# Layer 0's x_proj product ahead of TensorE's other work in slot 6, and three PSUM banks for the first image of the last layer

## The chip, the cores and the metric

The kernel runs on one core of one Trainium2 chip. A core has five engines that each work through their own queue in order: TensorE (PE in the profile, with its weight loads as PEld), VectorE (DVE), ScalarE (ACT), GpSimd (POOL) and SyncE (SP), which here only issues transfers between HBM and the on-chip memory SBUF. TensorE writes its results to PSUM[...]. The metric is the device time of one execution in microseconds; lower is better. Before the change it is 8299.07 us, the median of three runs (8296.89 to 8299.89).

## The reference

The network has four layers on four images of 64 x 64 positions with 128 channels, each of the form `x = x + layer(group_norm(x))`, all in float32. The change touches layer 0, a selective scan over the image in four directions k, and the beginning of layer 3, attention over a 7 x 7 neighbourhood. Layer 0, cut to what matters here:

```python
x_dbl = einsum('bkdl,kcd->bkcl', xs, x_proj_weight)          # x_proj: 256 channels -> 8 + 16 + 16
dts, Bm, Cm = split(x_dbl, [R, R + N], axis=2)               # R = 8, N = 16
delta = softplus(einsum('bkrl,kdr->bkdl', dts, dt_projs_weight) + bias)
A = -exp(A_logs)
def step(h, xs):                                             # 4096 steps, 16 states for each channel
    ut, dt, bt, ct = xs
    h = exp(dt[..., None] * A) * h + (dt * ut)[..., None] * bt[:, :, None, :]
    return h, einsum('bkdn,bkn->bkd', h, ct)
```

Layer 3: `qkv = x @ qkv_w.T + qkv_b` on the normalised image, then for every position the softmax over its 49 neighbours of `q . k * scale + bias`, the weighted sum of their `v`, and a projection.

## The kernel before

Layer 0 walks through 128 units (image b, direction k in the order 1, 3, 0, 2, chunk c of 512 positions), each of 16 slots, one for each state n. In a slot GpSimd makes `dB`, ScalarE makes the two halves of `dA`, VectorE runs the two scans, TensorE transposes a quarter of an older group of `h` into `pt`, ScalarE copies it to `hT`, and TensorE multiplies the `hT` of the slot before into `yT`. Here are the slot's loop, and the generator that prepares the next unit's delta:

```python
def inputs(k, c, u, par):
    xd_ps = spare("xd_ps")[0:48, :]
    for s in range(2):
        nc.tensor.matmul(xd_ps, lhsT=w_x[:, s, k, :], rhs=u[:, s, :], start=(s == 0), stop=(s == 1))
    yield
    xd = xds[c % 2]
    nc.scalar.copy(xd[0:24, :], xd_ps[0:24, :])
    yield
    Ct = tmp.tile([48, 32, 16], F32, name="Ct")[32:48]
    nc.scalar.copy(Ct, xd_ps[32:48, :].rearrange("n (a t) -> n t a", t=32))
    ...                                        # stores of xd and Ct to HBM
    yield bd, Wd
    ...                                        # delta: dp = w_dt . xd, exp, ln, min/max; du
spare = lambda name: psm.tile([P, CH], F32, name=name, tag="m")     # one bank, for all side work
...
for n in range(NS):
    slot = NS * i + n
    ...
    nc.gpsimd.tensor_tensor(dB, du, B_now[...], ALU.mult)
    flush("dve")
    if i + 1 < len(units) and n in (9, 11):
        next(coming)
    for s in range(2):
        dA = psx.tile([P, CH], F32, name="dA", tag="x")             # three banks
        nc.scalar.activation(dA, delta[:, s, :], AF.Exp, scale=A_neg[:, k, s, n : n + 1])
        nc.vector.tensor_tensor_scan(h[:, s, :, q], dA, dB[:, s, :], state[:, s, n : n + 1], ALU.mult, ALU.add)
        if s == 0 and i + 1 < len(units):
            if n in (7, 8, 10):
                next(coming)
        elif n == 7 and i + 1 < len(units):
            bd_next, Wd_next = next(coming)
        flush(f"act{s}")
    copy = transposed() if slot >= LAG else (lambda: None)          # LAG = 7
    copy()
    flush("act2")
    ...
    if i + 1 < len(units):
        if n == 1:
            u_next, v_next = fetch(*units[i + 1])
        if n == 6:
            coming = inputs(*units[i + 1][1:], v_next, (i + 1) % 2)
        if n in (6, 7, 9):
            next(coming)
        if n == 13:
            ready = next(coming)
```

What `transposed` puts into the queues: eight transposes, then the yT products of the slot before; the copy of `pt` comes last. `pt` has a single buffer (two banks).

```python
pt = ps.tile([P, 4, 2, P], F32, name="pt")
for j in range(4):
    for s in range(2):
        nc.tensor.transpose(pt[:, j, s, :], G["h"][...], sh.ident)
if todo is not None:
    products(*todo)                            # four products of hT (slot before) into yT
hT = tmp.tile([P, 4, 2 * P], F32, name="hT")
return lambda: nc.scalar.copy(hT, pt.rearrange("p j s d -> p j (s d)"))
```

Beside this the loop carries side work in small pieces: preparing the next image (norm, the z product, a 3 x 3 convolution as nine products) and finishing the last one. Its TensorE results go through the same spare bank, and its other parts are put off with `later`, to a place in a later slot; `flush` puts them into the queues there. The convolution starts in slot 11 and ends with its ninth product in slot 3 of the next unit. What follows it is `silu`, with `wait = (0, 1, 2)` for a convolution and `(0, 0, 1)` for z:

```python
def silu(v, bias, minus, dst, later, wait):    # v is the spare bank
    e = tmp.tile([P, CH], F32, name="e", tag="t2", bufs=4)
    def product():
        nc.vector.scalar_tensor_tensor(e, v, bias, e, ALU.add, ALU.mult)
        nc.sync.dma_start(dst, e)
    later("act0", nc.scalar.activation, e, v, AF.Exp, scale=-1.0, bias=minus)
    later("act1", nc.scalar.activation, e, e, AF.Ln, bias=1.0, slots=1 + wait[0])
    later("act0" if wait[1] else "act2", nc.scalar.activation, e, e, AF.Exp, scale=-1.0, slots=1 + wait[1])
    later("dve", product, slots=1 + wait[2])
    return e
```

So the `product` of a convolution is put into VectorE's queue at the head of slot 6. Behind it, in slot 7, ScalarE copies `e` by columns (`xw`).

Layer 2 takes its SBUF in pools that are stacked in the order of their creation, and layer 3's pools are stacked on the same addresses once layer 2 is done:

```python
pools = pool("l2big", 1), pool("l2tmp", 1), pool("l2small", 1), ps      # layer 2; big holds x, z, m, sp: 7 x 16 KB
...
wp = pool("l3w", 1)                            # layer 3: weights, two padded images kp, zero
big, tmp, small = pool("l3big", 2), pool("l3tmp", 2), pool("l3small", 4)
psS, psT = pool("l3psS", 2, space=PSUM), pool("l3psT", 2, space=PSUM)
psO, psM = pool("l3psO", 1, space=PSUM), pool("l3psM", 1, space=PSUM)
```

Layer 3 prepares an image in `front(b)`: transpose and statistics (`pg`), normalise, values (`pv`), keys (`pk`). Of the first image all pieces run before anything else; those of the others are spread over the attention steps of the image before. `queries` takes `pq` from the same bank.

```python
def front(b):
    x = big.tile([P, NJ, DM], F32, name="x3")
    load_image(nc, x, x_in(b))
    ...
    for c in range(NCH):
        pg = psM.tile([P, CH], F32, name="pg3", tag="m")
        for q in range(4):
            nc.tensor.transpose(pg[:, q * P : (q + 1) * P], x[:, 4 * c + q, :], sh.ident)
        nc.vector.bn_stats(st[:, c, :], pg)
        nc.scalar.copy(xn[:, c * CH : (c + 1) * CH], pg)
        yield
    s_, o_ = sh.group_scale(st, psM, small, "m")
    ...                                        # xn = xn * s_ + o_ in two halves on VectorE
    for c in range(NCH):
        pv = psM.tile([P, 4, P], F32, name="pv3", tag="m")
        ...                                    # four products xn . w_v
        vt = tmp.tile([P, 4, P], F32, name="vt")
        tt(vt, pv, w["v_b"].unsqueeze(1).to_broadcast([P, 4, P]), ALU.add)
        ...                                    # two stores of vt into the padded v in HBM
        yield
    for c in range(NCH):
        pk = psM.tile([P, CH], F32, name="pk3", tag="m")
        nc.tensor.matmul(pk, lhsT=w["qkv"][:, P : 2 * P], rhs=xn[:, c * CH : (c + 1) * CH], start=True, stop=True)
        nc.scalar.activation(kps[b % 2][...], pk.rearrange("p (h w) -> p h w", w=64), AF.Identity, bias=...)
        yield
...
for _ in front(0):
    pass
rows = {0: queries(0, 0)}
for s in range(NU + 6):                        # attention steps; ps = psS.tile([P, 2, CH]) from step 0 on
    ...
```

Of the kernel before, what the change touches and what calls it, by code (L numbers as in the profile page):

```python
# [2 lines left out]

# [7 lines left out]
F32 = mybir.dt.float32  # L11
# [5 lines left out]
P = 128  # L17
# [5 lines left out]
CH = 512  # L23
# [59 lines left out]
def layer0(sh, A, x_in, x_out, scr):  # L83
# [7 lines left out]
    with ExitStack() as ctx:  # L91
        pool = lambda name, bufs, **kw: ctx.enter_context(tc.tile_pool(name=name, bufs=bufs, **kw))
        wp = pool("l0w", 1)
        tmp = pool("l0tmp", 2)
        small = pool("l0small", 2)
# [361 lines left out]
        with tc.manual_schedule(engines=order):  # L457
            for i, (b, k, c) in enumerate(units):
                if i % per == 0:
                    ln_st = small.tile([P, NJ, 1, 6], F32, name="ln_st")  # L460
                    if b + 1 < NB:
                        sides.insert(0, Side(before(b + 1, spare, later), 17 + 8 * 23, NS * i, 28 * NS))
                rev = k >= 2
                pc = NCH - 1 - c if rev else c
                dst = lambda n, pc=pc, b=b: tiles(scr(f"y2{b % 2}" if n == 2 else f"y{n}")[pc * CH : (pc + 1) * CH, :])
                delta, du = ready
                if c == 0:
                    state = small.tile([P, 2, NS], F32, name="state")
                    nc.gpsimd.memset(state, 0.0)
                unit = dict(k=k, rev=rev, pc=pc, u=u, yT=[None, None], started=set(), st=ln_st, dst=dst)  # L470
                Ws = unit["Ws"] = {}
                coming = None
                for n in range(NS):
                    slot = NS * i + n
                    g, q = divmod(n, 4)
                    if q == 0:
                        B_now = Bb
                        if g < 3:
                            Bb = broadcast(bd, g + 1)
                        elif i + 1 < len(units):  # L480
                            Bb = broadcast(bd_next, 0)
                        h = tmp.tile([P, 2, CH, 4], F32, name="h", bufs=3)
                        G = dict(unit=unit, g=g, h=h, q=0)
                    dB = tmp.tile([P, 2, CH], F32, name="dB", bufs=3)
                    nc.gpsimd.tensor_tensor(dB, du, B_now[:, q : q + 1, :].to_broadcast([P, 2, CH]), ALU.mult)  # L485
# [4 lines that stand above are left out]
                        dA = psx.tile([P, CH], F32, name="dA", tag="x")  # L490
                        nc.scalar.activation(dA, delta[:, s, :], AF.Exp, scale=A_neg[:, k, s, n : n + 1])  # L491
                        nc.vector.tensor_tensor_scan(  # L492
                            h[:, s, :, q], dA, dB[:, s, :], state[:, s, n : n + 1], ALU.mult, ALU.add
# [4 lines that stand above are left out]
                        elif n == 7 and i + 1 < len(units):  # L498
                            bd_next, Wd_next = next(coming)
                        flush(f"act{s}")  # L500
                    copy = transposed() if slot >= LAG else (lambda: None)
                    copy()
                    flush("act2")
                    if q == 2:
                        W = Ws[g] = tmp.tile([P, 32, 16], F32, name="W", bufs=4)
                        nc.sync.dma_start(W, Wd[g, 0 : P * CH].rearrange("(p t a) -> p t a", p=P, a=16))
                    if q == 3:
                        queue.append(G)
                        if c < NCH - 1:
                            later("act1", nc.scalar.copy, state[:, :, 4 * g : 4 * g + 4], h[:, :, CH - 1, :], slots=5)  # L510

                    if i + 1 < len(units):
                        if n == 1:
                            u_next, v_next = fetch(*units[i + 1])
                        if n == 6:
                            coming = inputs(*units[i + 1][1:], v_next, (i + 1) % 2)
                        if n in (6, 7, 9):
                            next(coming)
                        if n == 13:
                            ready = next(coming)  # L520

                    if n == 10:
                        y = unit["y"] = tmp.tile([P, 4, 2 * P], F32, name="y", tag="t4", bufs=4)
                        if k == 0:
                            src = scr("y3").rearrange("(w q r) d -> r w q d", w=64, r=2)
                            for r in range(2):
                                nc.sync.dma_start(y[64 * r : 64 * r + 64], src[r, :, 4 * c : 4 * c + 4, :])
                        elif k != 1:
                            nc.sync.dma_start(y, dst(1 if k == 3 else 0))

                    inside = [d for d in sides if d.inside]
                    free = n not in BUSY and not inside and slot >= taken
                    able = dict(f=False, l=False, m=free, n=free and n != 5, z=free and n != 5, c=free and n == 11)
                    for d in inside or [d for d in sides if able[d.need] and d.due(slot)][:1]:
                        taken = slot + dict(m=1, n=2, z=2, c=3)[d.need]
                        d.free_at = slot + 1
                        d.step()
                    for d in sides:
                        if d.need in ("f", "l") and d.due(slot):
                            if d.need == "l":  # L540
                                d.free_at = slot + 3
                            d.step()
                    sides = [d for d in sides if d.need]
                if i + 1 < len(units):
                    u, bd, Wd = u_next, bd_next, Wd_next
                if i % per == per - 1:
                    slot += 1
                    if b + 1 < NB:
                        for d in sides:
                            d.finish(flush_all)  # L550
                    if b + 1 < NB:
                        sides = [Side(after(b, ln_st, later, range(NCH)), 8 * 6, NS * (i + 1) + 8, (28 if b + 2 < NB else 22) * NS)]
                elif b == NB - 1 and i % per == 3 * per // 4:

                    done = [NS * (i + 1 + n) + 8 for n in range(NCH)]
                    sides.append(Side(after(b, ln_st, later, range(NCH - 1, -1, -1)), 8 * 6, done[0], 1, done))
            while queue or copied:
                transposed()()
            for d in sides:
                d.finish(flush_all)  # L560
# [816 lines left out]
def layer2(sh, w, wp, x_in, x_out, scr, wt):  # L1377
    tc, nc = sh.tc, sh.nc
    with ExitStack() as ctx:
# [5 lines left out]
                nc.vector.memset(t, 0.0)  # L1385
        for t in w["XG"]:
            nc.vector.memset(t[:, 4, 64:65], 1.0)
        pools = pool("l2big", 1), pool("l2tmp", 1), pool("l2small", 1), ps
        paced = copy(sh)
        paced.nc = Pace(nc)  # L1390
        engines = {mybir.EngineType.PE, mybir.EngineType.Activation, mybir.EngineType.DVE, mybir.EngineType.Pool}
# [12 lines left out]
def layer3(sh, A, x_in, out, v_pads):  # L1404
# [5 lines left out]
    with ExitStack() as ctx:  # L1410
# [31 lines left out]

        def front(b):

            x = big.tile([P, NJ, DM], F32, name="x3")
            load_image(nc, x, x_in(b))
            xn = big.tile([P, NT], F32, name="xn3")
# [1 line left out]
            yield  # L1449
            st = small.tile([P, NCH, 6], F32, name="gn_st", bufs=2)  # L1450
            for c in range(NCH):
                pg = psM.tile([P, CH], F32, name="pg3", tag="m")
                for q in range(4):
                    nc.tensor.transpose(pg[:, q * P : (q + 1) * P], x[:, 4 * c + q, :], sh.ident)
                nc.vector.bn_stats(st[:, c, :], pg)
                nc.scalar.copy(xn[:, c * CH : (c + 1) * CH], pg)
                yield
# [4 lines left out]
                nc.vector.tensor_scalar(xc, xc, s_, o_, ALU.mult, ALU.add)  # L1462
            yield
            for c in range(NCH):
                pv = psM.tile([P, 4, P], F32, name="pv3", tag="m")
                for q in range(4):
                    nc.tensor.matmul(
                        pv[:, q, :],
# [9 lines left out]
                    nc.sync.dma_start(rows[r], vt[64 * r : 64 * r + 64])  # L1478
                yield
            for c in range(NCH):  # L1480
                pk = psM.tile([P, CH], F32, name="pk3", tag="m")
                nc.tensor.matmul(
                    pk, lhsT=w["qkv"][:, P : 2 * P], rhs=xn[:, c * CH : (c + 1) * CH], start=True, stop=True
                )
                nc.scalar.activation(
                    kps[b % 2][:, 3 + 8 * c : 11 + 8 * c, 3:67],
                    pk.rearrange("p (h w) -> p h w", w=64),
                    AF.Identity,
                    bias=w["qkv_b"][:, 1:2],
                )  # L1490
                yield
# [343 lines left out]
```

## Time and profile before

| stage | from, us | to, us | PE busy, us | DVE busy, us | ACT busy, us | POOL busy, us | granted PE clock |
|---|---|---|---|---|---|---|---|
| layer 0 | 0 | 5938 | 4719 | 5382 | 5287 | 5127 | 0.98 |
| end of layer 0 | 5938 | 6046 | 67 | 74 | 66 | 61 | 0.88 |
| layer 1 | 6046 | 6640 | 515 | 302 | 151 | 0 | 0.91 |
| layer 2 | 6640 | 7692 | 764 | 565 | 340 | 101 | 0.82 |
| entry of layer 3 | 7692 | 7777 | 45 | 15 | 11 | 2 | 0.50 |
| layer 3 | 7777 | 8299 | 462 | 415 | 374 | 191 | 0.97 |

The table is the profile's busy time by window, with the windows set at the first and last instructions of the layers. In every profile line below, `L379` is a line of the kernel, `pt<-ident,h` says what is written and what is read, `x8` is how many instructions the line sums up, and what stands in brackets or behind the bar is how long the engine sat idle just before it and who ended that. The idle time of an engine that isn't the bound costs nothing. So the reading goes from the engine that is busiest in a stage to what it waits for, and from there to the order of the queues.

### The profile page before, as it was taken

What the parts mean: (1) busy time and instruction counts of PE and PEld (TensorE: products, weight loads), DVE (VectorE), ACT (ScalarE), POOL (GpSimd) and SP (SyncE); (2) the same over time, 40 slices, a digit from 0 to 9 for tenths busy, and PEclk for the clock granted to TensorE, in tenths of its full rate; (3) what the DMA queues carried; (4) which work ended last, traced back from release to release, by engine and by line L of the source; (5) the groups of instructions that cost most, each with busy time, mean ns of one, the idle gap of its engine ahead of it and who ended that gap; (6) DMA issues with size and microseconds to landing.
All of it is one profiled execution on the core that took longest, in us unless ns stands there. A gap on an engine that the chain in (4) does not pass through costs nothing.

```text
span 8299.4 us, 140501 instructions
## 1 busy us (share of the span) xinstructions
PE 6571.5 (79%) x52976; PEld 4171.0 (50%) x52976; DVE 6753.8 (81%) x7948; ACT 6229.0 (75%) x10246; POOL 5482.7 (66%) x2502
## 2 busy tenths in 40 slices
PE   7788888778788877888877777787779878686689
PEld 3444454444445444444544444454467766464456
DVE  2889999998999999889999999999944545645578
ACT  3899999989899898989988999999822213315467
POOL 0889889988888898888889999999800011020233
PEclk9899999999999999999999999999989988788799
DMA  6445555445555544455555445455442041331332
GB/s 127 153 143 188 162 164 176 158 156 166 176 168 172 173 165 161 157 169 168 176 179 170 157 156 185 174 174 181 148 103 43 23 118 35 87 101 31 96 94 79
DMA packets 1281977, 1163.78 MB, mean 140 GB/s; under 512 B 637973, under 2 KB 1075825, under 8 KB 1214354
## 3 DMA queue, kind: packets, MB, share of 16 engines
q1 hardware_dynamic: 1279618, 1153.06, 44.0%
q8 instruction: 417, 6.83, 0.3%
q14 instruction: 262, 2.15, 0.1%
q10 hardware_dynamic: 1680, 1.74, 0.1%
HBM read 962.66 MB, written 189.74 MB: 139 GB/s over the span
## 4 chain that ended last, share of the span: by engine, by line
PE 21%; ACT 11%; DVE 11%; issue 3%; DMA 2%; POOL 2%; SPq 1%; DVEq 0%; ACTq 0%; POOLq 0%
DVE h L492 4%; ACT hT L389 4%; ACT dA L491 4%; PE pt L379 2%; PE po L695 1%; PE pf L690 1%; POOL dB L485 1%; PE pz L883 1%; PE pu L883 1%; PE pt L1518 1%; DVE in_st L883 1%; PE pb L883 1%; DVE m L883 1%; PE pa L883 1%; PE ps L1572 1%
## 5 line engine op out<-in xcount | busy, mean ns | idle before, releaser
L492 DVE TENSOR_TENSOR_SCAN h<-dA,state,dB 128x512 f32<-128x512 f32 x4096 | 4958.8, 1269 | 361.5 <-ACT dA L491 247.2
L485 POOL TENSOR_TENSOR dB<-du,Bb 128x1024 f32<-128x1024 f32 x2048 | 4817.0, 2385 | 550.7 <-DVE h L492 381.9
L379 PE MATMUL pt<-ident,h 128*128 128x128 f32 x16384 | 2249.0, 281 | 1014.9 <-ACT hT L389 1010.0
L379 PEld LDWEIGHTS pt<-ident,h 128*128 128x128 f32 x16384 | 1838.5, 143 | 2051.6 <-ACT hT L389 1806.4
L491 ACT ACTIVATE dA<-delta,A_neg 128x512 f32<-128x512 f32 x4096 | 2746.1, 690 | 163.8 <-DVE h L492 140.8
L389 ACT COPY hT<-pt 128x1024 f32<-128x1024 f32 x2048 | 2068.3, 1010 | 176.9 <-PE pt L379 163.4
L414 PE MATMUL yT<-hT,W 128*32 128x256 f32 x16384 | 1396.9, 414 | 2.7 <-DVE y L430 2.1
L883 POOL COPY XG<-Xs 64x9 f32<-64x9 f32 (+2 forms) x44 | 10.9, 292 | 1020.8 <-ACT Xs L883 1020.7
L414 PEld LDWEIGHTS yT<-hT,W 128*32 128x32 f32 x16384 | 454.4, 150 | 352.0 <-issue 336.9
L214 PE MATMUL cv<-xn,taps 128*128 128x512 f32 x1152 | 612.8, 632 | 0.0
L1556 POOL TENSOR_TENSOR S<-S,sm 128x784 f32<-128x784 f32 x128 | 191.1, 1493 | 403.1 <-DVE sm L1554 251.9
L325 PE MATMUL dp<-xd,w_dt 65*128 65x512 f32 x512 | 298.1, 665 | 103.9 <-ACT Ct L312 91.8
L334 POOL TENSOR_TENSOR du<-delta,u 128x1024 f32<-128x1024 f32 x128 | 305.1, 2383 | 67.6 <-DVE delta L331 67.6
L214 PEld LDWEIGHTS cv<-xn,taps 128*128 128x128 f32 x1152 | 183.4, 188 | 234.0 <-issue 232.6
L306 PE MATMUL xd_ps<-u,w_x 128*48 128x512 f32 x512 | 251.8, 615 | 40.9 <-DMA u<-l_xw 16.8
L1563 ACT ACTIVATE S<-S,mx 128x196 f32<-128x196 f32 x512 | 227.9, 448 | 33.0 <-DVE mx L1590 32.4
L691 ACT ACTIVATE h<-pf,b 128x512 f32<-128x512 f32 x128 | 88.0, 687 | 146.7 <-PE pf L690 146.7
L331 DVE SCALAR_TENSOR_TENSOR delta<-delta,dp 128x512 f32<-128x512 f32 x256 | 169.2, 661 | 25.7 <-ACT delta L329 25.7
L325 PEld LDWEIGHTS dp<-xd,w_dt 65*128 65x128 f32 x512 | 79.4, 195 | 219.5 <-ACT Ct L312 150.4
L1432 POOL MEMSET kp<- 128x210 f32 (+1 forms) x8 | 1.8, 286 | 275.0 <-DMA x<-m 275.0
L328 ACT ACTIVATE delta<-dp 128x512 f32<-128x512 f32 x256 | 152.4, 595 | 28.4 <-PE dp L325 23.8
L329 ACT ACTIVATE delta<-delta 128x512 f32<-128x512 f32 x256 | 162.3, 634 | 8.1
(335 smaller groups left out, 7183.8 us busy)
## 6 DMA issues: line engine op xcount, KB each, us to landing
Bb<-l_B SPq DMA_DIRECT2D x512, 1024.0 KB
W<-l_W SPq DMA_DIRECT2D x512, 256.0 KB
l_y<-y SPq DMA_DIRECT2D x128, 512.0 KB
u<-l_xw SPq DMA_DIRECT2D x64, 512.0 KB
y<-l_y SPq DMA_DIRECT2D x64, 512.0 KB
u<-l_xr SPq DMA_DIRECT2D x64, 512.0 KB
V<-l_v SPq DMA_DIRECT2D x512, 49.0 KB
wr<-wt SPq DMA_DIRECT2D x128, 136.0 KB
```

The source lines that it names most:

```text
L214: nc.tensor.matmul(pm, lhsT=taps[:, s, t, :], rhs=xn[:, dy : dy + 8, dx : dx + 64], start=(t == 0), stop=(t == 8),)
L306: nc.tensor.matmul(xd_ps, lhsT=w_x[:, s, k, :], rhs=u[:, s, :], start=(s == 0), stop=(s == 1))
L325: nc.tensor.matmul(dp, lhsT=w_dt[:, k, s * P : (s + 1) * P], rhs=xd, start=True, stop=True)
L334: nc.gpsimd.tensor_tensor(du, delta, u, ALU.mult)
L379: nc.tensor.transpose(pt[:, j, s, :], G["h"][:, s, t0 : t0 + 32, :].rearrange("p t n -> p (t n)"), sh.ident)
L389: return lambda: nc.scalar.copy(hT, pt.rearrange("p j s d -> p j (s d)"))
L414: nc.tensor.matmul(U["yT"][e][32 * jo : 32 * jo + 32, qo % 2, :], lhsT=U["Ws"][G["g"]][:, :, 4 * q + j], rhs=hT[:, j, :], start=((e, jo) n ...
L485: nc.gpsimd.tensor_tensor(dB, du, B_now[:, q : q + 1, :].to_broadcast([P, 2, CH]), ALU.mult)
L491: nc.scalar.activation(dA, delta[:, s, :], AF.Exp, scale=A_neg[:, k, s, n : n + 1])
L492: nc.vector.tensor_tensor_scan(h[:, s, :, q], dA, dB[:, s, :], state[:, s, n : n + 1], ALU.mult, ALU.add)
L883: r = f(*args, **kw)
L1563: nc.scalar.activation(Sn, Sn, AF.Exp, bias=U["mx"][:, n : n + 1], accum_out=sm[:, n : n + 1])
```

## The change

In layer 0 the first piece of `inputs`, the x_proj product of the next chunk (`xd_ps`), is moved within slot 6: from the end of the slot, behind TensorE's transposes and yT products, to a place ahead of them. All its other pieces stay in their slots. It is meant to have the product done when ScalarE wants to copy it in slot 7. In layer 3 the products and transposes of the first image's `front` take three banks in turn instead of one: the bank of `psM` and the first bank of each of the two `psS` buffers, which no attention step uses yet. The pools of layer 2 are created in another order, tmp, small, big, so that layer 3's first tiles lie at other tiles' addresses. No arithmetic is added or taken away.

```diff
--- before.py
+++ after.py
@@ -1,3 +1,4 @@
+import itertools
 from contextlib import ExitStack
 from copy import copy
 
@@ -498,6 +499,9 @@
                         elif n == 7 and i + 1 < len(units):
                             bd_next, Wd_next = next(coming)
                         flush(f"act{s}")
+                    if n == 6 and i + 1 < len(units):
+                        coming = inputs(*units[i + 1][1:], v_next, (i + 1) % 2)
+                        next(coming)
                     copy = transposed() if slot >= LAG else (lambda: None)
                     copy()
                     flush("act2")
@@ -512,9 +516,7 @@
                     if i + 1 < len(units):
                         if n == 1:
                             u_next, v_next = fetch(*units[i + 1])
-                        if n == 6:
-                            coming = inputs(*units[i + 1][1:], v_next, (i + 1) % 2)
-                        if n in (6, 7, 9):
+                        if n in (7, 9):
                             next(coming)
                         if n == 13:
                             ready = next(coming)
@@ -1385,7 +1387,8 @@
                 nc.vector.memset(t, 0.0)
         for t in w["XG"]:
             nc.vector.memset(t[:, 4, 64:65], 1.0)
-        pools = pool("l2big", 1), pool("l2tmp", 1), pool("l2small", 1), ps
+        tmp, small, big = pool("l2tmp", 1), pool("l2small", 1), pool("l2big", 1)
+        pools = big, tmp, small, ps
         paced = copy(sh)
         paced.nc = Pace(nc)
         engines = {mybir.EngineType.PE, mybir.EngineType.Activation, mybir.EngineType.DVE, mybir.EngineType.Pool}
@@ -1442,6 +1445,13 @@
 
         def front(b):
 
+            ring = itertools.count()
+
+            def bank(name):
+                if b == 0 and next(ring) % 3:
+                    return psS.tile([P, 2, CH], F32, name="ps3")[:, 0, :]
+                return psM.tile([P, CH], F32, name=name, tag="m")
+
             x = big.tile([P, NJ, DM], F32, name="x3")
             load_image(nc, x, x_in(b))
             xn = big.tile([P, NT], F32, name="xn3")
@@ -1449,7 +1459,7 @@
             yield
             st = small.tile([P, NCH, 6], F32, name="gn_st", bufs=2)
             for c in range(NCH):
-                pg = psM.tile([P, CH], F32, name="pg3", tag="m")
+                pg = bank("pg3")
                 for q in range(4):
                     nc.tensor.transpose(pg[:, q * P : (q + 1) * P], x[:, 4 * c + q, :], sh.ident)
                 nc.vector.bn_stats(st[:, c, :], pg)
@@ -1462,7 +1472,7 @@
                 nc.vector.tensor_scalar(xc, xc, s_, o_, ALU.mult, ALU.add)
             yield
             for c in range(NCH):
-                pv = psM.tile([P, 4, P], F32, name="pv3", tag="m")
+                pv = bank("pv3").rearrange("p (q d) -> p q d", q=4)
                 for q in range(4):
                     nc.tensor.matmul(
                         pv[:, q, :],
@@ -1478,7 +1488,7 @@
                     nc.sync.dma_start(rows[r], vt[64 * r : 64 * r + 64])
                 yield
             for c in range(NCH):
-                pk = psM.tile([P, CH], F32, name="pk3", tag="m")
+                pk = bank("pk3")
                 nc.tensor.matmul(
                     pk, lhsT=w["qkv"][:, P : 2 * P], rhs=xn[:, c * CH : (c + 1) * CH], start=True, stop=True
                 )
```

## The prediction

> **What bounds the kernel now.** I read the page first (busy shares, then the costliest groups), then the idle time by stage, then the instruction timeline of one slot of layer 0 and of the entry into layer 3. From the page:
>
> ```profile
> PE 6571.5 (79%) x52976; PEld 4171.0 (50%) x52976; DVE 6753.8 (81%) x7948; ACT 6229.0 (75%) x10246; POOL 5482.7 (66%) x2502
> L492 DVE TENSOR_TENSOR_SCAN h<-dA,state,dB 128x512 f32<-128x512 f32 x4096 | 4958.8, 1269 | 361.5 <-ACT dA L491 247.2
> L379 PE MATMUL pt<-ident,h 128*128 128x128 f32 x16384 | 2249.0, 281 | 1014.9 <-ACT hT L389 1010.0
> L389 ACT COPY hT<-pt 128x1024 f32<-128x1024 f32 x2048 | 2068.3, 1010 | 176.9 <-PE pt L379 163.4
> ```
>
> Read the second line as: VectorE runs 4096 scans, 4958.8 us in all, and sat idle 361.5 us just before them, 247.2 us of it until ScalarE delivered a dA. All 4096 lie in layer 0, which by the stage windows takes 5938 us of the 8299. The next two lines are a loop of two engines: the transposes wait for the copy hT to empty `pt`, and the copy waits for the transposes. One turn costs 1.09 + 1.01 us plus two hand-overs, about 2.26 us, against 2.37 us for two scans. So VectorE bounds a quiet slot and the loop of TensorE and ScalarE lies only 0.1 us behind it. Sorted by slot (index of the scan in the trace, two a slot, sixteen slots a unit), the idle time before scans is 55.3 us in slot 7, 98.4 in slot 8, 54.4 in slot 10, 40.3 in slot 5, and little elsewhere. That is where the x_proj product sits:
>
> ```profile
> L306 PE MATMUL xd_ps<-u,w_x 128*48 128x512 f32 x512 | 251.8, 615 | 40.9 <-DMA u<-l_xw 16.8 <-DVE gn_st L170 13.9 <-DVE e L230 9.1
> L309 ACT COPY xd<-xd_ps 24x512 f32<-24x512 f32 x128 | 74.2, 580 | 123.9 <-PE xd_ps L306 123.9
> ```
>
> ScalarE waits 123.9 us, nearly 1 us a unit, for the product (four TensorE instructions, 1.92 us). The change goes after this wait. Now one such slot, unit 50 of 128, in the timeline (start, length, engine):
>
> ```profile
> 2511.79 1.09 PE L379 MATMUL pt<-ident,h 128*128 128x128 f32 x8 [0.98 <-ACT hT L389]
> 2512.72 0.74 DVE L230 SCALAR_TENSOR_TENSOR e<-cv,cols,e 128x512 f32<-128x512 f32 x1
> 2512.81 0.67 PE L414 MATMUL yT<-hT,W 128*32 128x256 f32 x8
> 2512.97 1.01 ACT L389 COPY hT<-pt 128x1024 f32<-128x1024 f32 x1
> 2513.38 3.62 DVE L492 TENSOR_TENSOR_SCAN h<-dA,state,dB 128x512 f32<-128x512 f32 x3
> 2513.52 1.92 PE L306 MATMUL xd_ps<-u,w_x 128*48 128x512 f32 x4
> 2513.88 0.70 ACT L491 ACTIVATE dA<-delta,A_neg 128x512 f32<-128x512 f32 x1
> 2515.36 1.09 PE L379 MATMUL pt<-ident,h 128*128 128x128 f32 x8
> 2515.47 0.58 ACT L309 COPY xd<-xd_ps 24x512 f32<-24x512 f32 x1 [0.89 <-PE xd_ps L306]
> 2517.73 1.28 DVE L492 TENSOR_TENSOR_SCAN h<-dA,state,dB 128x512 f32<-128x512 f32 x1 [0.72 <-ACT dA L491]
> ```
>
> The line to notice is the second. VectorE's product `e` reads a convolution out of the spare bank, the one bank that xd_ps needs too, and it ends at 2513.46; the x_proj product starts at 2513.52.
>
> The entry into layer 3, same view:
>
> ```profile
> 7689.11 0.36 SPq L883 DMA_DIRECT2D x<-m  x1
> 7692.36 0.35 SPq L1423 DMA_DIRECT2D qkv<-in_qkv_w  x1
> 7704.34 1.09 PE L1454 MATMUL pg<-ident,x 128*128 128x128 f32 x4 [32.63 <-DMA x<-x]
> 7728.76 2.05 PE L1467 MATMUL pv<-qkv,xn 128*128 128x128 f32 x8 [2.28 <-DVE xn L1462]
> 7777.44 3.85 PE L1572 MATMUL ps<-kp,q 32*64 32x196 f32 x48 [0.87 <-ACT q L1500]
> ```
>
> From layer 2's last store to the first attention product 88 us pass, and every engine waits on the next through one bank.
>
> [...] the transposes of slot 7 start at 2515.36, when the product has been issued, though `pt` was free from 2513.98. So whatever x_proj waits for, the transposes behind it wait for too. [...] In the trace each copy of pg by ScalarE starts 0.08 us after VectorE's statistics of it end. [...] in the trace the granted clock is 0.50 from 7692 to 7777, and a 512-wide pair takes 2.08 us there and 1.13 us at 7781.
>
> **Layer 0: a unit with a convolution in the bank.** No work is added; the order on TensorE becomes product, transposes, yT products. In unit 50 the product can start no earlier than now (2513.5, behind `e`). The transposes follow 1.84 us later (2515.36, as slot 7's do now), the copy hT 1.18 us after that (2516.55, now 2512.97), the next dA 0.91 us later (2517.45, now 2513.88), and the xd copy, no longer waiting, 0.66 us later (2518.1, now 2515.47). Everything behind it on ScalarE moves by 2.6 us. VectorE has its stock of dA used up by 2515.8 (it runs the two scans of slot 6), and in the profile it is already waiting for ScalarE behind this point (0.72 us, then 0.44 and 0.41). So the 2.6 us reach the scans in full.
>
> **The other units.** I read the same four times off the trace for each of 126 units: end of the yT products of slot 5, end of the last reader of the spare bank, start of slot 6's transposes, start of the xd copy. New shift = (new start of the transposes) + 2.74 us − (old start of the xd copy). It is charged only where the scans behind it wait for dA today, or where dA comes later than the scan's own start.
> - Bank held into slot 6, direction k other than 1: 51 units, 2.5 us each, +127 us.
> - Bank held, k = 1: 16 units. `e` ends earlier (0.43 us after the transposes' old start), 2.0 us each, +32 us.
> - Bank free, k = 1: 15 units. TensorE idles 1.6 us before its transposes, the product fits in, the wait goes: −0.67 us each, −10 us.
> - Bank free, others: 44 units. TensorE idles 0.56 to 0.98 us there, transposes come 0.8 to 1.2 us later, 0.8 to 0.9 us of wait go; about 0, +2 us.
>
> Sum: +151 us. The held ones are convolutions of the next image, whose `e` falls in slot 6 by the schedule, and single z products and norm statistics.
>
> **Layer 3's entry.** Three banks: today a pg step takes 2.52 us (transposes 1.1, statistics 0.70, copy 0.58, one after the other), and a pv or pk step 2.86 us. With three banks a step costs what its slowest engine takes: about 1.15 us for pg, 2.1 us for pv (half clock, and two vt buffers whose stores take about 4 us a round), 1.2 to 2.1 us for pk. So pv, pk and the first pq shrink from 48.7 to some 32 us: −17 us. The pool order: layer 3's weights and x lie at the addresses of layer 2's first pools. Today that is `big`, which holds m until its last store lands at 7692.3. With tmp and small first, sized from their tiles at about 67 and 15 KB a partition against 45 KB of layer 3 weights and kp, the weights and the first x lie where nothing is used after about 7610. If the load is issued early, pg follows VectorE's last work at 7689.1 and pv starts near 7703: −26 us, pg's gain included. If the queue keeps it behind the last store, pv starts near 7718: −11 us. I give the first 0.7, so −21 on average. At the entry to layer 2 the first image's load waits for layer 1's store (TensorE idle 14.5 us); moved to other addresses it may come some us earlier, −4.
>
> Sum: 151 − 17 − 21 − 4 = +109 us. I take 8 us off, for dA lost in slot 6 and made up elsewhere: 8299 + 101 = 8400 us.
>
> **Rivals.**
> - *The wait simply goes.* The 123.9 us would be saved and nothing delayed: with layer 3 about 8299 − 110 − 42 = 8147. For it: TensorE does idle before slot 6's transposes, 0.98 us in unit 50. Against it: the product takes 1.84 us, and in 67 of 126 units the bank isn't free then.
> - *Nothing moves in layer 0*, because VectorE bounds it and has scans in stock: 8299 − 42 = 8257. For it: in 19 free units of k = 2 no scan waits around slot 7. Against it: in the held units the scans of slots 7 and 8 wait for ScalarE already.
> - *More than my sum*: the delay also breaks ScalarE's lead for slots 9 to 11, where delta's two activations come. Then 3 to 4 us a held unit, 8299 + 230 − 42 = 8487.
>
> **Range and chances.** The layer 0 term carries the doubt: 151 us, give or take 50. The entry's 42 us may be 25 to 55. Hence 8325 to 8460. Two per cent slower is 8465, just beyond: 0.11. Faster by 2% would need 8133, which even the first rival doesn't reach: 0.01. Within 2%: 0.88.
>
> **What will show it.** In the changed profile: the wait of xd for xd_ps near zero; the copy hT and the idle of L379 waiting longer in slot 6; the product's own wait for VectorE's `e` in some 50 units, 2 to 3 us each; idle before scans up from 361.5 to about 500 us, in slots 7 and 8; layer 0 ending near 6090 instead of 5938; from layer 2's last vector work to the first ps some 45 us instead of 88. I am wrong if the idle before scans falls, which would mean that TensorE reaches slot 6 late enough for the bank to be free, or if x is still loaded after the last store of m.

## The result, and the profile after

The changed kernel takes 8486.67 us (median of 4 runs, 8482.33 to 8488.73) against 8299.48 us before: ratio 1.0224, 95% interval 1.0207 to 1.0242. It is slower by 187 us, and 27 us above the range I had given. The page of the changed kernel, the same rows as before (its lines have shifted by one in layer 0):

```profile
PE 6654.7 (78%) x52976; PEld 4209.6 (50%) x52976; DVE 6763.0 (80%) x7948; ACT 6217.8 (73%) x10246; POOL 5480.0 (65%) x2502
L493 DVE TENSOR_TENSOR_SCAN h<-dA,state,dB 128x512 f32<-128x512 f32 x4096 | 4967.9, 1271 | 568.0 <-ACT dA L492 439.8
L380 PE MATMUL pt<-ident,h 128*128 128x128 f32 x16384 | 2272.9, 283 | 940.8 <-ACT hT L390 936.8
L390 ACT COPY hT<-pt 128x1024 f32<-128x1024 f32 x2048 | 2068.1, 1010 | 519.5 <-PE pt L380 509.0
```

VectorE does the same scans in the same time (4967.9 us), but sits idle 568 us before them instead of 361.5, and the copy hT now waits 509 us for the transposes where it had waited 163. The product and the copy of xd, from the groups of the changed kernel:

```profile
L307 PE MATMUL xd_ps<-u,w_x 128*48 128x512 f32 x512 | 307.6, 733 | 206.4 <-DVE e L231 159.7 <-DMA u<-l_xw 17.1 <-DVE gn_st L171 14.5
L310 ACT COPY xd<-xd_ps 24x512 f32<-24x512 f32 x128 | 73.1, 571 | 16.8 <-PE xd_ps L307 16.8
```

The wait the change was after has gone: ScalarE waits 16.8 us for the product instead of 123.9. In its place TensorE waits 206 us ahead of the product, most of it for VectorE's `e`. The number I had not reckoned with stands in the middle: one product instruction takes 733 ns on average instead of 615, although it does the same work. One stage after the other, between the same instructions in both traces:

| stage | before, us | after, us | difference |
|---|---|---|---|
| layer 0, to the end of the last scan | 6006.7 | 6221.0 | +214.3 |
| layer 1, first transpose to last vector work | 586.0 | 591.7 | +5.7 |
| entry of layer 2, to its first transpose | 8.6 | 4.8 | −3.8 |
| layer 2, to its last vector work | 1044.5 | 1054.5 | +10.0 |
| entry of layer 3, to the first ps | 88.4 | 43.6 | −44.8 |
| layer 3, to the end | 522.0 | 527.7 | +5.7 |

The bodies of layers 1, 2 and 3 do the same in both kernels. In the twelve kernels run below, these bodies measured 585 to 591, 1042 to 1050 and 518 to 530 us without a pattern, so I read nothing into the rows of layers 1 and 3; the new addresses in layer 2 are tried alone below.

Unit 50 again, now in the changed kernel (timeline: start, length, engine, work, idle time before it):

```profile
2605.41 1.09 PE L380 MATMUL pt<-ident,h 128*128 128x128 f32 x8 [1.43 <-ACT hT L390]
2609.00 0.75 DVE L231 SCALAR_TENSOR_TENSOR e<-cv,cols,e 128x512 f32<-128x512 f32 x1
2609.66 2.45 DVE L493 TENSOR_TENSOR_SCAN h<-dA,state,dB 128x512 f32<-128x512 f32 x2
2609.80 2.59 PE L307 MATMUL xd_ps<-u,w_x 128*48 128x512 f32 x4 [2.71 <-DVE e L231]
2612.32 1.97 PE L380 MATMUL pt<-ident,h 128*128 128x128 f32 x8
2614.38 1.01 ACT L390 COPY hT<-pt 128x1024 f32<-128x1024 f32 x1 [5.17 <-PE pt L380]
2615.29 0.70 ACT L492 ACTIVATE dA<-delta,A_neg 128x512 f32<-128x512 f32 x1
2615.92 0.57 ACT L310 COPY xd<-xd_ps 24x512 f32<-24x512 f32 x1
2616.09 1.28 DVE L493 TENSOR_TENSOR_SCAN h<-dA,state,dB 128x512 f32<-128x512 f32 x1 [3.98 <-ACT dA L492]
```

The chain runs as I had drawn it: `e`, product, transposes, copy, dA, scan. But the product takes 2.59 us instead of 1.92 and the transposes behind it 1.97 instead of 1.09, and the scan is idle 3.98 us. The windows view of the changed kernel says why (stretch, length, busy time of PE, PEld, DVE, ACT and POOL, then the granted TensorE clock, the busy share of DMA and its GB/s):

```profile
2607.20:2609.70 2.50, 0.00 (x0) 0.00 (x0) 2.50 (x5) 2.02 (x3) 2.00 (x3) 1.00 0.00 0
2609.80:2612.30 2.50, 2.50 (x4) 0.41 (x4) 2.31 (x2) 0.00 (x0) 1.24 (x2) 0.72 0.27 105
2612.40:2614.20 1.80, 1.80 (x8) 1.49 (x8) 0.00 (x0) 0.00 (x0) 1.80 (x1) 0.50 0.00 0
2857.50:2861.10 3.60, 3.59 (x5) 0.65 (x5) 2.33 (x2) 0.00 (x0) 2.34 (x2) 0.50 0.19 73
```

First TensorE does nothing for 2.5 us. Then, in the middle of the product, the clock falls to half, and the transposes run at 0.50. The last row is the product of unit 55, at half clock throughout these 3.6 us.

The entry into layer 3, timeline of the changed kernel, and last what SyncE waited for (in total, how often, longest). The first value product, pv, now stands under the name `ps`, because it got one of the two new banks:

```profile
7908.09 7.81 SPq L885 DMA_DIRECT2D x<-m  x3
7918.93 9.92 SPq L722 DMA_DIRECT2D x<-x  x8
7923.02 1.09 PE L1464 MATMUL pg<-ident,x 128*128 128x128 f32 x4 [24.88 <-DMA x<-x]
7934.66 2.08 PE L1477 MATMUL ps<-qkv,xn 128*128 128x128 f32 x8 [2.13 <-DVE xn L1472]
7959.20 1.58 PE L1582 MATMUL ps<-kp,q 32*64 32x196 f32 x32 [0.87 <-ACT q L1510]
SPq L722 <- DMA x<-m: 2.7, 1, 2.7
```

The weights are no longer between the last store of m and the load of x, but x is still sent only when that store has landed (VectorE's last work ends at 7915.5). From pg to pv 11.6 us pass instead of 24.4, from pv to the first attention product 24.5 instead of 48.7.

### The profile page after: what moved, and what is told of

It reads as the page before. It is cut to its first block, busy times and chain, and to the rows that moved or that the text cites. A ratio compares the mean times of both kernels' runs of the same rounds, so it can differ in the third digit from the quotient of the medians.

```text
span 8486.9 us, 140244 instructions
## 1 busy us (share of the span) xinstructions
PE 6654.7 (78%) x52976; PEld 4209.6 (50%) x52976; DVE 6763.0 (80%) x7948; ACT 6217.8 (73%) x10246; POOL 5480.0 (65%) x2502
## 5 line engine op out<-in xcount | busy, mean ns | idle before, releaser
L493 DVE TENSOR_TENSOR_SCAN h<-dA,state,dB 128x512 f32<-128x512 f32 x4096 | 4967.9, 1271 | 568.0 <-ACT dA L492 439.8
L380 PE MATMUL pt<-ident,h 128*128 128x128 f32 x16384 | 2272.9, 283 | 940.8 <-ACT hT L390 936.8
L380 PEld LDWEIGHTS pt<-ident,h 128*128 128x128 f32 x16384 | 1858.8, 144 | 2011.2 <-ACT hT L390 1741.6
L307 PE MATMUL xd_ps<-u,w_x 128*48 128x512 f32 x512 | 307.6, 733 | 206.4 <-DVE e L231 159.7
L307 PEld LDWEIGHTS xd_ps<-u,w_x 128*48 128x48 f32 x512 | 60.1, 138 | 360.0 <-DVE e L231 186.8
L329 ACT ACTIVATE delta<-dp 128x512 f32<-128x512 f32 x256 | 152.4, 595 | 25.4 <-PE dp L326 20.5
L1528 PE MATMUL pt<-ident,S 128*98 128x128 f32 x1024 | 165.8, 286 | 3.3 <-POOL S L1566 1.9
```

The source lines that it names most:

```text
L380: nc.tensor.transpose(pt[:, j, s, :], G["h"][:, s, t0 : t0 + 32, :].rearrange("p t n -> p (t n)"), sh.ident)
L1528: nc.tensor.transpose(pt[:, half, hp, :], U["S"][:, e, hp, 98 * half : 98 * half + 98], sh.ident)
```

## The experiments

My theory had two parts. The move makes TensorE wait for the bank; and the wait is dearer than its length, because the clock falls and what stands behind it runs at half speed. The rival was the third of the prediction: 3.7 us a held unit because ScalarE loses its lead for the slots with delta's activations. A second rival put part of the 214 us down to the other SBUF addresses. Each ratio is against the kernel before, on the same chip.

**The move alone.** Only the moved product of the change's diff, nothing in layers 2 and 3.

> The x_proj product moved, nothing else of the change. Layer 0 grows by 214 us in the changed kernel's profile, against 151 us in my sum. If the move alone does this, this kernel is at 8299 + 214 = 8513 us, and slower than the whole change, whose entry into layer 3 gives some 45 us back. Rival: part of the 214 us comes from the other two parts (other SBUF addresses); then this one stays near 8299 + 151 = 8450 us.

8533.89 us, ratio 1.0282 (1.0262 to 1.0301), or 235 us more, and 21 us above my 8513. So the addresses have no part in the 214 us, and the move costs more than the whole change.

**The move, with TensorE kept busy.** In 45 of the units in which a convolution or z product holds the bank:

```diff
+ if n == 6 and i in HELD:
+     spin = ps.tile([P, 4, 2, P], F32, name="pt")
+     for r in range(2):
+         nc.tensor.matmul(spin[:, 2 * r : 2 * r + 2]..., lhsT=sh.ident, rhs=delta[:, r, :], start=True, stop=True)
  if n == 6 and i + 1 < len(units):
      coming = inputs(...)
      next(coming)
```

> The move, and in 45 units in which the bank is held by a convolution or z product (k not 1) two more matmuls of 512 columns ahead of it, into pt, read by nobody: 1.7 us of TensorE work in the time in which it waits for VectorE's e. Clock theory: the 60 us by which the held units came out dearer than my sum is TensorE falling to half clock during that wait (the product then takes up to 3.65 us instead of 1.92, the transposes 1.97 instead of 1.09); kept busy, it stays at full clock, and this kernel, with more work, is 40 to 60 us FASTER than the move alone. Rival (ScalarE's lead is lost for longer than I counted, the clock is a bystander): the spinning changes nothing or costs up to 45 x 0.1 = 5 us.

8461.05 us, ratio 1.0196 (1.0179 to 1.0212). It does 90 useless products more and is 73 us faster than the move alone. Unit 50 in its timeline, TensorE alone:

```profile
2592.89 1.98 PE L505 MATMUL pt<-delta,ident 128*128 128x512 f32 x4 [0.97 <-ACT hT L389]
2594.80 1.92 PE L306 MATMUL xd_ps<-u,w_x 128*48 128x512 f32 x4
2596.65 1.09 PE L379 MATMUL pt<-ident,h 128*128 128x128 f32 x8
```

The product is back at 1.92 us and the transposes at 1.09, and the clock granted in the product (2594.8 to 2596.7) is 1.00, where the changed kernel has 0.72. Nothing else about the order was changed, so the clock theory stands. (The two profiled runs differ by 63 us, 61 of them in layer 0.) Unit by unit, from the start of a slot 5 scan to the next unit's, against the kernel before:

| units | my sum, us | whole change, us | move alone, us | move and spin, us | products over 2.1 us: before / whole change / spin |
|---|---|---|---|---|---|
| 51, bank held, k not 1 | +127 | +187 | +187 | +131 | 0 / 35 / 2 |
| 16, bank held, k = 1 (not spun) | +32 | +34 | +44 | +34 | 1 / 9 / 7 |
| 15, bank free, k = 1 | −10 | −9 | −10 | −9 | 1 / 1 / 1 |
| 44, bank free, others | +2 | +6 | +5 | +8 | 1 / 2 / 2 |

The first row splits by the clock within the changed kernel too: its 35 units with a product over 2.1 us cost 4.2 us each, the other 16 cost 2.6, next to the 2.5 of my sum.

**A free bank.** The convolution's silu is drawn together so that `e` comes a slot earlier. First with the move, then, as a control, without:

```diff
- ..., later, (0, 1, 2))
+ ..., later, (0, 0, 1))
```

> The move, and the convolution's silu drawn together so that its product e is put into VectorE's queue in slot 5 instead of slot 6 (all three activations in slot 4): the spare bank is free when the x_proj product comes. Bank theory: it is the wait for the bank, not the place ahead of the transposes, that costs; about 36 of 45 units lose their 3 to 5 us, leaving single z products and norm statistics: 8299 + 40 us, give or take 30. Order rival: the transposes behind a 1.9 us product cost in any case; then it stays above 8299 + 120 us.

> Control for the one above: the kernel before with only the earlier silu. Both theories: within 20 us of before. What the move does with a free bank is the difference of the two.

With the move 8334.00 us, ratio 1.0034 (1.0021 to 1.0048); without it 8293.98 us, ratio 0.9995 (0.9988 to 1.0001). So the move costs 235 us with the bank as it was and 40 us with the bank mostly free: it is the bank. What is left can be read from the two profiles, over the same 51 units as above: in 10 of them TensorE still idles 1.7 to 4.4 us before the product, and these cost 34.7 us against the control; in the other 41 it idles 1.0 us at most, and together they cost nothing (−0.7 us). So the transposes behind a product that does not wait cost nothing there.

**The product between transposes and yT products.** `transposed` takes it as an argument and calls it after the eight transposes:

```diff
+ if between is not None:
+     between()                  # the x_proj product
  if todo is not None:
      products(*todo)
```

> The product between the transposes and the yT products of slot 6, everything else as before: it comes 0.6 us earlier, and nothing that the copy hT needs stands behind it. If delaying the transposes is what made the move dear, this costs nothing: free units of k = 1 and the convolutions of k = 1 gain 0.6 us each, 8299 - 19 = 8280 us. If any earlier place is dear because TensorE then waits for the bank, it is above 8320.

8261.28 us, ratio 0.9952 (0.9937 to 0.9967). An earlier place is not dear in itself; it is dear where the transposes stand behind the product's wait. The gain is 37 us against my 19. In the profile the 31 units of k = 1, where I expected it, gave 15 us; another 26 came from the others. The time at half clock between the first and the last scan fell as well, from 230 to 116 us; no run separates that.

**The same wait, from ScalarE's side.** TensorE's order is that of before; in slot 7 the copy of xd goes behind the second dA.

```diff
  if s == 0 and i + 1 < len(units):
-     if n in (7, 8, 10):
+     if n in (8, 10):
          next(coming)
  elif n == 7 and i + 1 < len(units):
+     next(coming)
      bd_next, Wd_next = next(coming)
```

> The kernel before, its TensorE order unchanged; instead ScalarE's order in slot 7: the copy of xd goes behind the second dA, so that ScalarE does 0.69 us of due work where it waited 0.8 to 0.9 us for the product. It goes after the same wait as the change, from the side of the waiting engine. Theory (the wait costs where ScalarE leads no more, in the held units and those of k = 1): about 82 units by 0.65 us, 8299 - 50 = 8249 us. Rival (the scans have stock, the wait is hidden): within 15 us of before.

8213.64 us, ratio 0.9888 (0.9868 to 0.9907), a gain of 85 us. Its scans and its copy of xd, from the groups:

```profile
L492 DVE TENSOR_TENSOR_SCAN h<-dA,state,dB 128x512 f32<-128x512 f32 x4096 | 4952.3, 1272 | 280.1 <-ACT dA L491 136.6 <-POOL dB L485 91.9 <-issue 32.5
L309 ACT COPY xd<-xd_ps 24x512 f32<-24x512 f32 x128 | 73.5, 575 | 19.4 <-PE xd_ps L306 18.1
```

ScalarE's wait goes from 123.9 to 18.1 us, as low as in the changed kernel, and the idle time before scans falls to 280.1 us instead of rising. The time at half clock between the first and last scan, summed from the trace, also falls, from 230 to 85 us (in the changed kernel 431). That may be why it gains more than I expected; no run separates it.

**The parts of layers 2 and 3.** The pool order alone, the banks alone, both, and both with

```diff
+ xs3 = pool("l3x", 2)
  wp = pool("l3w", 1)
  ...
- x = big.tile([P, NJ, DM], F32, name="x3")
+ x = xs3.tile([P, NJ, DM], F32, name="x3")
```

> The kernel before with layer 2's pools in the new order alone. In the changed kernel the weights of layer 3 came early, but the first x was still sent after the last store of m (wait of SyncE for it 2.7 us). If the order gives what the changed profile shows at its two places: about 4 us at the entry of layer 2 and 8 us at that of layer 3, so 8287 us. As I predicted it (x early) it would be 8299 - 19 = 8280. Rival: layer 2 itself grew by 10 us in the changed profile; if the new addresses did that, this kernel is no faster, 8297 or more.

> The kernel before with the three banks alone. From the changed profile: pg to pv 24.4 to 11.6 us less the share of the late loads, pv to the first ps 48.7 to 24.5: 8299 - 33 = 8266 us. Rival (the stores of vt or the load of x pace it anyway): 8280 or more.

> Both, without the move: the whole change minus layer 0's part. If the parts add up: 8299 - 47 = 8252 us, and the whole change is this plus the move's 235 us. If layer 2's 10 us belong to the new addresses they are missing here: 8262.

> The one above, and the x tiles of layer 3 get a pool of their own, created first, so that they lie at the lowest addresses, those of layer 2's tmp, and not behind the 45 KB of weights. If x came late in the changed kernel because its tile still lay on layer 2's small or big tiles, it is now there before VectorE's last work, and another 8 us go: 8244 us. If the load keeps its place in SyncE's queue behind the stores of m: no change.

On the chip of these four the kernel before takes 8303.73 us. Pool order: 8291.51 us, ratio 0.9985 (0.9976 to 0.9993). Banks: 8264.58 us, 0.9962 (0.9947 to 0.9977). Both: 8255.03 us, 0.9946 (0.9932 to 0.9961). The parts add up, layer 2 takes 1044.6 us with the new addresses, as before, and the whole change (+187) is the move's +235 and these −49 us. With x in a pool of its own: 8253.73 us, ratio 0.9940 (0.9923 to 0.9957), which can't be told from the one without. Its queue of SyncE:

```profile
7620.49 9.54 SPq L721 DMA_DIRECT2D x<-x  x7
...
7683.61 0.35 SPq L1426 DMA_DIRECT2D qkv<-in_qkv_w  x1
```

So x does come some 60 us early once its tile lies low enough: it was the address, not the queue. Which tile of layer 2 lay there is not shown. But now it is the statistics on VectorE that wait, behind layer 2's last work. From that work to pv 15.0 us pass instead of 19.5; the 8 us that I expected were 4.5, and the spread of the other stages hides them.

**What the runs favour, together.** Product where it was, earlier silu, later xd, pool order, banks, x in its own pool; and the same without the later xd.

> All that the runs favour: product where it was, earlier silu, xd behind the second dA, pool order, three banks, x of layer 3 in a pool of its own. If the gains add up: 8299 - 10 (silu) - 50 (xd) - 49 (entry) = 8190 us. If earlier silu and later xd take away the same wait, some 20 us less: 8210.

> The same without the later xd: 8299 - 10 - 49 = 8240 us. Its difference from the one above is what the later xd is worth beside the others.

8164.03 us, ratio 0.9831 (0.9816 to 0.9846), and 8242.36 us, ratio 0.9929 (0.9913 to 0.9944). The first beats both kernels, 135 us under the one before. The later xd is worth 78 us in it, nearly what it is worth alone, so the other changes don't take its gain away.

## Why the prediction was wrong

- **The direction and the path held.** A wait of VectorE for dA took the place of the one removed, by way of the bank and the order of TensorE's queue. The free units came out as summed (+2 and −10 us predicted, +6 and −9 measured). The held ones of k = 1 did so by luck (+32, measured +34): nine with a slow product cost 3.0 us each and seven without 1.0, against my 2.0, and in the move alone, with twelve slow ones, they measure +44.
- **The term that failed is the largest: "Bank held into slot 6, direction k other than 1: 51 units, 2.5 us each, +127 us".** It measured 187 us, 3.7 a unit. The step that failed is the length of the product and of the transposes behind it: I had charged 1.84 and 1.09 us, the durations of a TensorE at full clock, and at the same time had TensorE wait 2 to 3 us ahead of them. In 35 of the 51 units the clock fell to half (0.50 to 0.79 on average over the product) and the product took up to 3.65 us, the transposes up to 1.97. With the wait filled, the same term measures 131 us: the chain was right, the durations in it were not. I had reckoned with half clock for the entry of layer 3 alone, where the trace before shows 0.50. In the 35 units TensorE's wait ahead of the product was 2.11 to 4.39 us, in 22 of them 2.7.
- **The 8 us that I took off** for dA made up elsewhere don't show: with the wait filled, the four rows add up to some 165 us, above my 151.
- **The range was too narrow for its own terms.** A layer 0 of 201 us and an entry of 25 give 8299 + 201 − 25 − 8 = 8467, and the third rival stood at 8487; I had closed it at 8460.
- **The third rival had the number** (8487 us, 3 to 4 us a held unit) **and the wrong reason.** It said that ScalarE's lead is lost for slots 9 to 11. Idle time before scans in slot 10 is 54 us before and 55 after; the whole rise is in slot 7, from 55 to 264 us.
- **Against the second rival:** the stock of scans covered nothing in the held units; where the clock stayed up, 2.6 us of delay arrived for the 2.5 that I had counted.
- **The entry of layer 3 came out as summed, −45 us against −38, by other shares.** The early x, to which I gave 0.7, did not come. My working placed it behind 45 KB of weights, where nothing is used after about 7610; in the trace it waited for the last store of m, and with its tile moved down it came. For a late x I had −11 us up to pv; −20.5 was measured, 7.8 of it because the weights no longer load ahead of x. The step from pv to the first ps gained 24 us instead of 17. On the way TensorE was granted more of its clock, 0.84 on average instead of 0.50, and a pk pair took 1.13 us where I had charged a step 1.2 to 2.1.
- **A slip without weight:** only the first of the eight copies of pg starts 0.08 us after VectorE's statistics; the others start 0.03 us after them.

## What to carry to other kernels

Before an instruction is moved ahead in an engine's queue, look up what it has to wait for at its new place, its output's bank included. Here what stood behind it waited as well: in unit 50 of the changed kernel the transposes start at 2612.32, behind the product, though `pt` was free from 2608.02. Nor did the durations of the old trace hold behind TensorE's waits: in 35 of 51 units, with waits of 2.11 to 4.39 us, the clock fell to half. So don't reckon with those durations alone. It can be cheaper to leave the producer where it is and to give the waiting engine other due work first (here 85 us).

## What the runs showed that I had not expected

Useless work made a kernel faster: 90 products that nobody reads took 73 us off 8534, by keeping TensorE's clock up through waits of some 2.7 us (in unit 50 it was granted 1.00 in the product, against 0.72 in the changed kernel).

Not every such wait costs the clock: of 51 held units in the changed kernel, 35 had a product of more than 2.1 us and 16 had none (granted clock 1.00 over the product). The length of TensorE's wait alone doesn't tell them apart. It was 2.11 to 4.39 us in the 35 and 1.10 to 3.48 us in the 16; of the 30 waits of 2.7 us, 22 are among the 35 and 8 among the 16. All six above 3.5 us are among the 35, all four below 2 us among the 16. None of the runs was made to separate them further.

In the entry of layer 3, being busy for most of the time did not bring the clock back. Before the change TensorE was busy 35.3 of the 48.7 us from pv to the first attention product (by the ends that the profile models), and was granted half its clock throughout; in the 12.6 us behind it, 9.8 of them busy, it was granted 0.87. In the changed kernel the same step, 19.9 of 24.6 us busy, was granted 0.84.
